# Two-layer graph kernel: tile order at the start, PE transposes for every second node tile, and the MLP's input transposed by DMA as 16-bit halves

## Chip, cores and metric

The kernel runs on one core of one Trainium2 chip. The metric is device time in microseconds (us) of a whole launch; the time before is the median of three runs. The profile is of one further execution of the same program, taken by the hardware profiler. Engines are named as in the profile: PE (TensorE; PEld its weight loads), DVE (VectorE), ACT (ScalarE), POOL (GpSimd), SP (SyncE, which here only issues DMAs).

## What is computed

There are 3327 nodes with 1024 features each, and a weighted adjacency matrix. Cut to what matters, the reference is:

```python
# layer 0: quantised graph convolution
h = relu(layernorm(x))
xq = round(min(h / act_alpha, 1) * 15)
wq = round(clip(((W - mean(W)) / std(W)) / wgt_alpha, -1, 1) * 7)
s = relu(xq @ wq * scale)
x1 = x + scale2 * (adj / adj_scaling_factor) @ round(min(s / act_alpha2, 1) * 15)
# layer 1: graph attention with 8 heads of 64, then an MLP
h = relu(layernorm(x1)); Wh = h @ W_head            # per head
e = leaky_relu(Wh @ a1 [:, None] + Wh @ a2 [None, :], 0.2)
enc = concat_heads(elu(softmax(where(adj > 0, e, -9e15)) @ Wh))     # 3327 x 512
out = x1 + (relu(relu(relu(enc @ W1.T + b1) @ W2.T + b2) @ W3.T + b3) @ W4.T + b4)
```

## The kernel before

The nodes are cut into T = 26 tiles of 128 rows (the last one is short and padded). Each tile lies with its nodes in the 128 partitions, and the kernel runs through four stages, one after the other, with little overlap at the seams.

**First stage (L210 to L450): `xq @ wq`.** `x` comes in by DMA, two tiles to a buffer (`xs`, three buffers). DVE takes a tile's mean and variance (`bn_stats`, L239), a short chain of tiny instructions makes the scale and bias (`normalise`, L258; sqrt on ACT, for later tiles the small products on POOL), ACT normalises, applies relu and rounds to bytes (`to_bytes`, xb, L279), and DVE clamps to a bf16 tile xq (L289). As PE contracts over partitions, xq must be turned so that features lie in the partitions: this is `quantise`. For tile 0 eight PE transposes go into PSUM (L297) and ACT copies them out to `xqt` (L298); for the other 25 tiles SP issues one SBUF-to-SBUF DMA transpose (L300). PE multiplies `xqt` with the quantised weight `w_int` (L423, 16 matmuls of 128x512 to a tile), ACT evicts the result with relu and rounding (sb, L449), and DVE clamps it (s_int, L450). The result's PSUM tiles (mm) have three buffers.

The weight itself must be quantised first. That is a chain: statistics of its eight row blocks (six blocks on DVE at L334, two on ACT at L252 to L256), an aggregate (L359), two tiny matmuls with ones for the mean and the variance over all partitions (L361, L371), a square root on ACT, scale and bias (L162, L163). Then 16 half blocks are rounded to bytes by ACT (L408) or DVE (L406) and clamped by DVE (L412) or POOL (L410). Between those half blocks the program slips the steps of tiles 1 to 5, by the table `between` (L389).

**What sets the order.** Tile's scheduler puts the instructions of each engine in a fixed order when the kernel is built, by its own estimate of when each is ready, and each engine then runs its list in that order; every wait in such a list holds what stands behind it. Instructions given to `tc.keep_in_program_order` (`pin` in the listing) keep their order among themselves. Before, the small steps of `reciprocal`, `scaled` and `normalise` for tile 0 (L112, L117, L131 to L163) are not pinned, and they stand between or behind the weight's first statistics on DVE.

**Second stage (L453 to L555):** adjacency times `s_int`, layer norm, and per tile the heads' products `Wh`. **Third stage (L565 to L854): attention.** For each of 32 rounds (half of the nodes, head; `attends`) DVE builds 0/1 selections `sel` (L826), PE multiplies them with the features (acc, L835) and, between, mask times difference features (mps, L636), whose masks ACT casts (mf, L635) and whose PSUM bank (one buffer) ACT empties (part, L640). The generator `close` finishes a round some steps later, in pieces: adding, scaling, elu; its last piece is a DVE instruction (L697) that leaves 7 (or 6) tiles by 64 columns of `enc` in `ht`, which a DMA on POOL's queue (L701) writes to `enc_d` in DRAM as float32.

**MLP (L738 to L918).** It runs in groups of four tiles, 512 nodes wide (six groups of four and one of two). `load_nodes` (L761) loads a group's `enc` and `x1` with nodes in the partitions, into one of two buffers (nodes0, nodes1), a group ahead. PE transposes `enc` (16 transposes of 128x128 float32, L894), ACT evicts them to `enct` (L897), and three `dense` layers follow (L869, evicted by ACT at L876), then the last layer (o, L906), to which DVE adds `x1` and the bias (L902, L916), and SP stores (L918). Group 0's transposes (L783, L788) and first layer (L793, L801) are slipped into the last attention round by `first_layer`; its weights and biases are loaded there too (L758, L773), into memory that the attention has freed.

Of the kernel before, what the change touches and what calls it, by code (L numbers as in the profile page):

```python
# [8 lines left out]
F32 = mybir.dt.float32  # L9
BF16 = mybir.dt.bfloat16  # L10
F32R = mybir.dt.float32r
U8 = mybir.dt.uint8
I8 = mybir.dt.int8
# [15 lines left out]
HD = 64  # L29
# [30 lines left out]
def two_layer_kernel(  # L60
# [39 lines left out]
    feat_d = dram.tile([T, NH, P, HW], F32, name="feat_d")  # L100
    dsum_d = dram.tile([T, NPAIR, P, HW], F32, name="dsum_d")
    src_d = [dram.tile([NH, len(sub) * P], F32, name=f"src_d{i}") for i, sub in enumerate(SUBS)]
    enc_d = dram.tile([NP, EMB], F32, name="enc_d")

    const.tile([P, 152], F32, name="gap")
    ndst = const.tile([P, T, NH], F32, name="ndst")
    ratio = const.tile([P, T, NH], F32, name="ratio")


    def reciprocal(t, name):  # L110
        r = const.tile([P, 1], F32, name=name)
# [46 lines left out]
    def scale_and_bias(rs, mean, n, factor, tag, engine=nc.vector):  # L158
# [17 lines left out]
    with tc.tile_pool(name="at", bufs=2, reuse_waits="tile") as atp:  # L176
# [34 lines left out]
        w = large(w_life, "w", [P, KF, F])  # L211
        with tc.tile_pool(name="s1", bufs=2, reuse_waits="tile") as s1, tc.tile_pool(
            name="s1_mm", bufs=3, space=PSUM, reuse_waits="tile"
        ) as mm_ps, tc.tile_pool(name="s1_tp", bufs=1, space=PSUM, reuse_waits="tile") as tp_ps:
# [69 lines left out]
            def quantise(t, xb=None, ordered=False):  # L284
                if xb is None:
                    xb = to_bytes(t, ordered)

                xq = s1.tile([P, F], BF16, name="xq")
                ins = nc.vector.tensor_scalar(xq, xb, QA, None, ALU.min)  # L289
                if ordered:  # L290
                    pin(ins)

                xqt = s1.tile([P, KF, P], BF16, name="xqt", bufs=4)
                if t == 0:
                    tp = tp_ps.tile([P, KF, P], BF16, name="tp")
                    for k in range(KF):
                        nc.tensor.transpose(tp[:, k, :], xq[:, k * P : (k + 1) * P], ident_b)  # L297
                    pin(nc.scalar.copy(xqt, tp))  # L298
                else:
                    nc.sync.dma_start_transpose(xqt, xq)  # L300
                return xqt
# [279 lines left out]
    with tc.tile_pool(name="sel", bufs=4, reuse_waits="tile") as selp, tc.tile_pool(  # L581
# [83 lines left out]
        def close(i):  # L665
# [23 lines left out]
            for b in range(nb):  # L689
# [11 lines left out]
            nc.gpsimd.dma_start(  # L701
                enc_d[sub[0] * P : (sub[-1] + 1) * P, h * HD : (h + 1) * HD].rearrange(
                    "(b p) d -> p b d", p=P
                ),
                ht[:, :nb],
            )

        def pin(ins):
            tc.keep_in_program_order(ins)
# [21 lines left out]
        for i, (c, g, e, si) in enumerate(attends):  # L731
            if i == len(attends) - 1:
# [4 lines left out]
                def nodes(name):  # L737
                    n = large(mlp, name, [P, T * HW])  # L738
                    return (
                        n[:, : 4 * EMB].rearrange("p (q e) -> p q e", q=4),  # L740
                        n[:, 4 * EMB : 4 * (EMB + F)].rearrange("p (q e) -> p q e", q=4),
                    )

# [11 lines left out]
                def weight(ap, k, m):  # L755
# [22 lines left out]
                def first_layer():  # L778

                    for k in range(EMB // P):  # L780
                        tp = m_ps.tile([P, 512], F32, tag="mps", name="tp0")
                        for q in range(4):
                            nc.tensor.transpose(  # L783
                                tp[:, q * P : (q + 1) * P],
                                enc_x1[0][0][:, q, k * P : (k + 1) * P],
                                ident,
                            )
# [69 lines left out]
    with tc.tile_pool(name="s4", bufs=2, reuse_waits="tile") as s4, tc.tile_pool(  # L857
# [23 lines left out]
        for g, t0 in enumerate(range(0, T, 4)):  # L881
            tiles = range(t0, min(t0 + 4, T))
            cols = len(tiles) * P
            enc, x1 = enc_x1[g % 2]
            if t0 + 4 < T:
                load_nodes((g + 1) % 2, t0 + 4)
            if g == 0:
                h1 = h1_0
            else:
                enct = s4.tile([P, EMB // P, 512], F32, name="enct")  # L890
                for k in range(EMB // P):
                    tp = ps_p.tile([P, 512], F32, tag="ps", name="tp4")
                    for q, t in enumerate(tiles):
                        nc.tensor.transpose(  # L894
                            tp[:, q * P : (q + 1) * P], enc[:, q, k * P : (k + 1) * P], ident
                        )
# [65 lines left out]
```

## Time and profile before

| | us |
|---|---|
| median of three runs | 2277.46 |
| lowest and highest run | 2276.98, 2278.27 |
| the profiled execution's own time | 2277.77 |
| its span (first to last instruction) | 2276.0 |
| first product of the first stage (L423) | 28.5 |
| last product of the first stage | 134.8 |
| start of group 1's transposes in the MLP (L894) | 2012.7 |

How to read it: times are in us from the span's start, unless marked ns. A line of the timeline is start, duration, engine, source line, operation, `out<-in` with shapes, how many, and in brackets the engine's idle time before it and what ended it. A line of the waits is who waited, for whom, then total us, number of times, and the longest. A line of the chain is start, duration and what ran; the chain is followed back from the last instruction through what released each step. The page's slices cut the span in 40 and give the busy share in tenths. A matmul's duration holds its latency, so two neighbours overlap; the distance of their starts tells what one costs.

### The profile page before, as it was taken

The page shows a single profiled execution, that of the slowest core. Times are in us where ns is not written, and L with a number is a line of the kernel's source. Part 1 is how long each engine was busy: PE and PEld are TensorE (multiplying, and loading weights), DVE is VectorE, ACT ScalarE, POOL GpSimd, SP SyncE. Part 2 cuts the span into 40 slices and gives each one's busy share as a digit, 9 for nine tenths or more (in the row PEclk, how much of TensorE's full clock was granted, in tenths as well). Part 3 has the DMA queues.
Part 4 walks back from the last instruction along what each step waited for, and adds up shares of the span by engine and source line. Part 5 has one row for each costly group of instructions (what it writes and reads, how often), then busy time and mean ns, then how long its engine had stood idle before and what let it go on. Part 6 is the DMA issues. An engine that isn't in the chain of part 4 may idle for free. (4 is left out here: it accounts for less than half of the span.)

```text
span 2276.0 us, 31632 instructions
## 1 busy us (share of the span) xinstructions
PE 2219.2 (98%) x12688; PEld 1772.3 (78%) x12696; DVE 1538.1 (68%) x1963; ACT 978.7 (43%) x1640; POOL 143.6 (6%) x241
## 2 busy tenths in 40 slices
PE   4999999999999999899999999999999999999998
PEld 1467777777777777589999999999999999744444
DVE  7745545555555455487999999999999999732211
ACT  5633333433343333346555555555555555311110
POOL 1300101011010111000000000000000000000000
PEclk9999999999999999999999999999999999999999
DMA  6854444454444544754233141654242422333311
GB/s 208 207 188 134 159 144 159 134 164 151 150 152 139 167 146 152 261 176 137 85 114 112 60 134 55 226 174 149 85 146 84 137 85 75 127 143 126 120 56 56
DMA packets 176579, 311.47 MB, mean 137 GB/s; under 512 B 36452, under 2 KB 117300, under 8 KB 176432
## 3 DMA queue, kind: packets, MB, share of 16 engines
q1 hardware_dynamic: 156648, 236.28, 32.0%
q0 software_dynamic: 19776, 73.17, 10.0%
q8 instruction: 99, 1.62, 0.3%
q14 instruction: 48, 0.39, 0.1%
q10 hardware_dynamic: 8, 0.00, 0.0%
HBM read 216.07 MB, written 86.79 MB: 133 GB/s over the span
## 5 line engine op out<-in xcount | busy, mean ns | idle before, releaser
L826 DVE SCALAR_TENSOR_TENSOR sel<-srow,ndst,mask 128x896 fp32r<-128x896 f32 (+1 forms) x832 | 864.1, 1080 | 51.4 <-PE acc L835 38.7
L636 PE MATMUL mps<-dw,mf 128*128 128x260 f32 x2704 | 454.9, 283 | 0.1
L532 PE MATMUL mm<-s_int,hi 128*128 128x512 f32 x1352 | 432.9, 399 | 0.0
L532 PE MATMUL mm<-s_int,lo 128*128 128x512 f32 x1352 | 421.8, 391 | 0.0
L835 PE MATMUL acc<-f_even,sel 128*128 128x260 f32 x2704 | 397.1, 284 | 0.1
L835 PE MATMUL acc<-f_odd,sel 128*128 128x260 f32 x2704 | 394.5, 286 | 0.0
L635 ACT CAST mf<-mask 128x1664 fp32r<-128x1664 uint8 x208 | 331.3, 1593 | 124.0 <-PE mps L636 101.2
L636 PEld LDWEIGHTS mps<-dw,mf 128*128 128x128 f32 x2704 | 378.2, 188 | 0.3 <-ACT part L640 0.3
L835 PEld LDWEIGHTS acc<-f_odd,sel 128*128 128x128 f32 x2704 | 352.8, 188 | 7.3 <-issue 3.4
L835 PEld LDWEIGHTS acc<-f_even,sel 128*128 128x128 f32 x2704 | 355.1, 188 | 2.9 <-ACT srct L489 0.3
L532 PEld LDWEIGHTS mm<-s_int,lo 128*128 128x128 f32 x1352 | 253.8, 188 | 57.6 <-issue 5.7
L532 PEld LDWEIGHTS mm<-s_int,hi 128*128 128x128 f32 x1352 | 252.1, 188 | 55.7 <-issue 5.7
L192 DVE TENSOR_SCALAR mk<-at 128x896 uint8<-128x896 f32 (+1 forms) x104 | 61.5, 593 | 257.2 <-DMA at<-in_adj_t 256.3
L187 ACT CAST hi<-at 128x896 fp32r<-128x896 f32 x104 | 92.6, 891 | 328.9 <-PE mm L532 294.8
L473 PE MATMUL whm<-whead,ht 128*128 128x512 f32 x416 | 187.1, 603 | 0.8 <-ACT ht L470 0.8
L906 PE MATMUL o<-weights,h 128*128 128x512 f32 x416 | 179.7, 592 | 0.0
L906 PEld LDWEIGHTS o<-weights,h 128*128 128x128 f32 x416 | 79.0, 190 | 99.1 <-issue 98.8
L473 PEld LDWEIGHTS whm<-whead,ht 128*128 128x128 f32 x416 | 77.5, 191 | 98.2 <-issue 88.1
L191 DVE TENSOR_TENSOR lo<-at,hi 128x896 fp32r<-128x896 f32 x104 | 106.6, 1025 | 58.9 <-ACT hi L187 49.4
L640 ACT COPY part<-mps 128x260 f32<-128x260 f32 x104 | 39.2, 377 | 221.5 <-PE mps L636 221.5
L916 DVE TENSOR_TENSOR yo<-o,nodes 128x1024 f32<-128x1024 f32 (+1 forms) x27 | 31.9, 1184 | 138.2 <-PE o L906 138.0
L423 PE MATMUL mm<-w_int,xqt 128*128 128x512 bf16 x408 | 95.4, 386 | 14.8 <-ACT sb L449 4.8
(154 smaller groups left out, 1519.7 us busy)
## 6 DMA issues: line engine op xcount, KB each, us to landing
feat_d<-fw POOLq DMA_DIRECT2D x26, 1040.0 KB, 5.4
f_even<-feat_d SPq DMA_DIRECT2D x7, 3380.0 KB, 13.3
f_odd<-feat_d SPq DMA_DIRECT2D x7, 3380.0 KB, 12.7
at<-in_adj_t SPq DMA_DIRECT2D x52, 448.0 KB, 4.4
at<-in_adj_t SPq DMA_DIRECT2D x52, 384.0 KB, 3.2
mask<-mask_d SPq DMA_DIRECT2D x39, 416.0 KB, 7.4
dw<-dsum_d SPq DMA_DIRECT2D x16, 910.0 KB, 8.8
dsum_d<-dw POOLq DMA_DIRECT2D x26, 520.0 KB, 6.5
```

The lines of the kernel that those rows point to most:

```text
L187: ins = nc.scalar.copy(hi, at)
L191: nc.vector.tensor_tensor(lo, at, hi.bitcast(F32), ALU.subtract)
L192: ins = nc.vector.tensor_scalar(mk[:, r], at, 0.0, None, ALU.is_gt)
L423: nc.tensor.matmul(mm[:, r], xqts[t][:, k, :], w_int[:, k, r], start=(k == 0), stop=(k == KF - 1))
L473: nc.tensor.matmul(whm, ht[:, k, :], whead[:, k, :], start=(k == 0), stop=(k == KF - 1))
L532: nc.tensor.matmul(mm[:, c * 512 : (c + 1) * 512], which[:, q, :], s_int[j][:, c * 512 : (c + 1) * 512], start=(j == 0 and which is hi), s ...
L635: nc.scalar.copy(mf, mask[:, j : j + TH, :])
L636: nc.tensor.matmul(ps, mf[:, j % TH, :], dw[:, j, :], start=(j == 0), stop=(j == T - 1))
L640: nc.scalar.copy(part[:, i % 7], ps.rearrange("p (q c) -> p q c", q=2))
L826: nc.vector.scalar_tensor_tensor(sel[:, :nb], srow[:, :nb], ndst[:, j, h : h + 1], mask[:, :, j, :], ALU.is_gt, ALU.mult,)
L835: nc.tensor.matmul(accs[b], sel[:, b, :], f[:, j, :], start=(j == 0), stop=(j == T - 1))
L906: nc.tensor.matmul(ps[:, c * 512 : (c + 1) * 512], h3[:, k, q * P : (q + 1) * P], w4[:, k, c * 512 : (c + 1) * 512], start=(k == 0), stop= ...
```

## The change

- In the first stage, `reciprocal` and `scaled` are pinned, tile 0's scale and bias are written out as pinned instructions ahead of the weight's statistics, and tile 0's rounding to bytes stands ahead of them too.
- Every tile with an even number is transposed by PE into PSUM and copied out by ACT (two PSUM buffers instead of one); the tiles with odd numbers keep the DMA transpose. The ACT copy is pinned where the tile's other steps are (tiles 0 and 2).
- `enc` goes to DRAM as two planes of 16-bit halves of its float32 words: one more ACT copy in `close` (eh) splits the words, and two DMAs on POOL's queue write them. In the MLP, SP loads each group by two DMA transposes, one of each plane, so that features come to lie in the partitions, and ACT joins the halves to words again: four copies to a group, made in the group before it; for group 0 in `first_layer`. PE's transposes of `enc` go.
- A constant gap in SBUF shrinks by the 32 words that the new small tiles take.

```diff
-    enc_d = dram.tile([NP, EMB], F32, name="enc_d")
-    const.tile([P, 152], F32, name="gap")
+    enc_d = dram.tile([2, NP, EMB], U16, name="enc_d")
+    const.tile([P, 120], F32, name="gap")
...
     def reciprocal(t, name):
-        nc.vector.reciprocal(r, t)
+        tc.keep_in_program_order(nc.vector.reciprocal(r, t))
...
     def scaled(t, c, name):
-        nc.vector.tensor_scalar(r, t, c, None, ALU.mult)
+        tc.keep_in_program_order(nc.vector.tensor_scalar(r, t, c, None, ALU.mult))
...
+    def halves_of_words(words):
+        return words.bitcast(U16).rearrange("p (n two) -> p two n", two=2)
...
-        ) as mm_ps, tc.tile_pool(name="s1_tp", bufs=1, ...) as tp_ps:
+        ) as mm_ps, tc.tile_pool(name="s1_tp", bufs=2, ...) as tp_ps:
...
-                if t == 0:
+                if t % 2 == 0:
                     tp = tp_ps.tile([P, KF, P], BF16, name="tp")
                     for k in range(KF):
                         nc.tensor.transpose(tp[:, k, :], xq[:, k * P : (k + 1) * P], ident_b)
-                    pin(nc.scalar.copy(xqt, tp))
+                    ins = nc.scalar.copy(xqt, tp)
+                    if ordered:
+                        pin(ins)
                 else:
                     nc.sync.dma_start_transpose(xqt, xq)
...
             r_aa = reciprocal(aa_t, "r_aa")
+            pin(nc.vector.tensor_scalar(mv0[:, 0, 1:2], mv0[:, 0, 1:2], EPS, None, ALU.add))
             to_q = scaled(r_aa, 2.0 * QA, "to_q")
-            normalise(xs01, mv0, 0, 1)
+            s0, q0, r0, b0 = (small.tile([P, 1], F32, name=f"x0{c}", bufs=1) for c in "sqrb")
+            v0 = mv0[:, 0, 1:2]
+            pin(nc.scalar.activation(s0, v0, AF.Sqrt))
+            pin(nc.vector.reciprocal(r0, s0))
+            pin(nc.vector.scalar_tensor_tensor(q0, v0, r0, s0, ALU.mult, ALU.add))
+            pin(nc.vector.reciprocal(r0, q0))
+            pin(nc.vector.tensor_scalar(r0, r0, to_q, None, ALU.mult))
+            pin(nc.vector.scalar_tensor_tensor(b0, mv0[:, 0, 0:1], -1.0, r0, ALU.mult, ALU.mult))
+            ready[0] = xs01[0], r0, b0
...
+            xb0 = to_bytes(0, ordered=True)
             weight_statistics(0)
-            xqts = {0: quantise(0, ordered=True)}
+            xqts = {0: quantise(0, xb0, ordered=True)}
...
-            nc.gpsimd.dma_start(enc_d[... rows of sub ..., h * HD : (h + 1) * HD], ht[:, :nb])
+            eh = s3.tile([P, 7, HD], F32, tag="ex", name="eh").rearrange("p b d -> p (b d)")
+            eh = eh.bitcast(U16).rearrange("p (q n) -> p q n", q=2)[:, :, : nb * HD]
+            nc.scalar.copy(eh, halves_of_words(ht[:, :nb].rearrange("p b d -> p (b d)")))
+            for q in range(2):
+                nc.gpsimd.dma_start(enc_d[q, ... rows of sub ..., h * HD : (h + 1) * HD], eh[:, q])
...
+                def by_feature(enc, cols):
+                    k = EMB // P
+                    return enc[:, :, : k * cols].rearrange("p q (k c) -> p q k c", k=k)
                 def load_nodes(i, t0):
-                    for q, t in enumerate(range(t0, min(t0 + 4, T))):
-                        nc.sync.dma_start(enc[:, q, :], enc_d[t * P : (t + 1) * P, :])
+                    rows = slice(t0 * P, min(t0 + 4, T) * P)
+                    for q in range(2):
+                        nc.sync.dma_start_transpose(by_feature(enc, rows.stop - rows.start)[:, q], enc_d[q, rows])
...
                 def first_layer():
                     for k in range(EMB // P):
-                        tp = m_ps.tile([P, 512], F32, tag="mps", name="tp0")
-                        for q in range(4):
-                            nc.tensor.transpose(tp[:, q * P : (q + 1) * P], ..., ident)
-                        nc.scalar.copy(enct0[:, k], tp)
+                        nc.scalar.copy(halves_of_words(enct0[:, k]), by_feature(enc_x1[0][0], 512)[:, :, k])
                         yield
...
+            enct = following if g else None
             if t0 + 4 < T:
                 load_nodes((g + 1) % 2, t0 + 4)
+                following = s4.tile([P, EMB // P, 512], F32, name="enct")
+                n = (min(t0 + 8, T) - t0 - 4) * P
+                for k in range(EMB // P):
+                    nc.scalar.copy(
+                        halves_of_words(following[:, k, :n]),
+                        by_feature(enc_x1[(g + 1) % 2][0], n)[:, :, k],
+                    )
             if g == 0:
                 h1 = h1_0
             else:
-                enct = s4.tile([P, EMB // P, 512], F32, name="enct")
-                for k in range(EMB // P):
-                    tp = ps_p.tile([P, 512], F32, tag="ps", name="tp4")
-                    for q, t in enumerate(tiles):
-                        nc.tensor.transpose(tp[:, q * P : (q + 1) * P], enc[:, q, k * P : (k + 1) * P], ident)
-                    nc.scalar.copy(enct[:, k, :cols], tp[:, :cols])
                 h1 = dense(enct, EMB // P, w1, bb1, D1 // P, cols, "h1")
```

More of the change, by code (lines that the diff above doesn't have):

```diff
@@ L12 @@
 U8 = mybir.dt.uint8
+U16 = mybir.dt.uint16
 I8 = mybir.dt.int8
@@ L213, in two_layer_kernel @@
             name="s1_mm", bufs=3, space=PSUM, reuse_waits="tile"
-        ) as mm_ps, tc.tile_pool(name="s1_tp", bufs=1, space=PSUM, reuse_waits="tile") as tp_ps:
+        ) as mm_ps, tc.tile_pool(name="s1_tp", bufs=2, space=PSUM, reuse_waits="tile") as tp_ps:
             w_int = s1.tile([P, KF, F], BF16, name="w_int", bufs=1)
@@ L700, in close @@
             )
[L701 to L706, printed above, removed]
+            eh = s3.tile([P, 7, HD], F32, tag="ex", name="eh").rearrange("p b d -> p (b d)")
+            eh = eh.bitcast(U16).rearrange("p (q n) -> p q n", q=2)[:, :, : nb * HD]
+            nc.scalar.copy(eh, halves_of_words(ht[:, :nb].rearrange("p b d -> p (b d)")))
+            for q in range(2):
+                nc.gpsimd.dma_start(
+                    enc_d[q, sub[0] * P : (sub[-1] + 1) * P, h * HD : (h + 1) * HD].rearrange(
+                        "(b p) d -> p b d", p=P
+                    ),
+                    eh[:, q].rearrange("p (b d) -> p b d", d=HD),
+                )
         def pin(ins):
@@ L739, in nodes @@
                     return (
-                        n[:, : 4 * EMB].rearrange("p (q e) -> p q e", q=4),
+                        n[:, : 4 * EMB].bitcast(U16).rearrange("p (q r) -> p q r", q=2),
                         n[:, 4 * EMB : 4 * (EMB + F)].rearrange("p (q e) -> p q e", q=4),
@@ L780, in first_layer @@
                     for k in range(EMB // P):
-                        tp = m_ps.tile([P, 512], F32, tag="mps", name="tp0")
-                        for q in range(4):
[L783 to L787, printed above, removed]
-                        nc.scalar.copy(enct0[:, k], tp)
+                        nc.scalar.copy(
+                            halves_of_words(enct0[:, k]), by_feature(enc_x1[0][0], 512)[:, :, k]
+                        )
                         yield
@@ L883, in two_layer_kernel @@
             cols = len(tiles) * P
-            enc, x1 = enc_x1[g % 2]
+            x1 = enc_x1[g % 2][1]
+            enct = following if g else None
             if t0 + 4 < T:
                 load_nodes((g + 1) % 2, t0 + 4)
+                following = s4.tile([P, EMB // P, 512], F32, name="enct")
+                n = (min(t0 + 8, T) - t0 - 4) * P
+                for k in range(EMB // P):
+                    nc.scalar.copy(
+                        halves_of_words(following[:, k, :n]),
+                        by_feature(enc_x1[(g + 1) % 2][0], n)[:, :, k],
+                    )
             if g == 0:
@@ L889, in two_layer_kernel @@
             else:
-                enct = s4.tile([P, EMB // P, 512], F32, name="enct")
-                for k in range(EMB // P):
-                    tp = ps_p.tile([P, 512], F32, tag="ps", name="tp4")
-                    for q, t in enumerate(tiles):
-                        nc.tensor.transpose(
-                            tp[:, q * P : (q + 1) * P], enc[:, q, k * P : (k + 1) * P], ident
-                        )
-                    nc.scalar.copy(enct[:, k, :cols], tp[:, :cols])
                 h1 = dense(enct, EMB // P, w1, bb1, D1 // P, cols, "h1")
```

## Prediction

> **What bounds the kernel now.** I read the page first (shares, slices), then the chain that ended last, then PE's waits by stage, then the timelines of the first 60 us and of the last 350 us. Line numbers are those of the kernel before.
>
> The page gives the span and says that TensorE is the bound: 98% busy, every slice but the first at 8 or 9 tenths.
>
> ```profile
> span 2276.0 us, 31632 instructions
> ...
> PE 2219.2 (98%) x12688; PEld 1772.3 (78%) x12696; DVE 1538.1 (68%) x1963; ACT 978.7 (43%) x1640; POOL 143.6 (6%) x241
> ...
> PE   4999999999999999899999999999999999999998
> ...
> DMA  6854444454444544754233141654242422333311
> ```
>
> So PE work that goes is worth its time, PE work that comes costs its time, and of waits only PE's count. In the first stage (L423, 28.5 to 134.8 us), from the waits of PE between 28 and 135 us (total us, times, longest):
>
> ```profile
> PE mm L423 <- ACT sb L449: 4.8, 5, 2.0
> PE mm L423 <- DVE w_int L412: 4.3, 3, 3.5
> PE mm L423 <- POOL w_int L410: 2.9, 5, 0.9
> PE mm L423 <- DMA xqt<-xq: 2.0, 2, 1.5
> ```
>
> The w_int waits are the quantisation of the weight (28.5 to 48 us). The rest, from 49.5 us on, is 1.5 (DMA) and 3.3 us (ACT; its fifth wait, 1.5 us, ends at 49.5). Ahead of that the timeline of all engines has the chain that starts the stage: tile 0's scale is late, so ACT's statistics of the weight are late, and DVE's aggregate at 22.48 waits for them.
>
> ```profile
> 13.00 0.14 DVE L163 SCALAR_TENSOR_TENSOR l01n<-mv,l01r 128x1 f32<-128x1 f32 x1
> ...
> 13.17 1.24 ACT L279 ACTIVATE xb<-xs,l01n,l01r 128x1024 uint8<-128x1024 f32 x1 [6.34 <-DVE l01n L163]
> ...
> 15.20 1.03 PE L297 MATMUL tp<-ident_b,xq 128*128 128x128 bf16 x8 [8.86 <-DVE xq L289]
> 16.27 1.01 ACT L298 COPY xqt<-tp 128x1024 bf16<-128x1024 bf16 x1 [1.85 <-PE tp L297]
> 17.18 1.06 ACT L252 ACTIVATE junk<-w 128x1024 bf16<-128x1024 f32 x1
> ...
> 22.48 0.51 DVE L359 BATCH_NORM_AGGREGATE w_mv<-w_stats 128x2 f32<-128x78 f32 x1 [3.77 <-ACT junk L256]
> ```
>
> The MLP is PE alone. The chain that ended last (start, us, what) has in each group 1.75 us of transposes, then 17.54 and 27.47 us of products:
>
> ```profile
> 2012.83 1.75 PE tp L894 x16
> 2014.58 17.54 PE h_ps L869 x40
> 2032.12 27.47 PE o L906 x64
> ...
> 2246.61 0.87 PE tp L894 x8
> ```
>
> **What the Trainium skill says.** (1) "ScalarE: Activation LUTs", What ACT_TABLE_LOAD costs: an ACTIVATE with immediates takes 186 ns + 0.833 ns per element, overlapping the next by about 93 ns. The trace agrees: 1012 ns for 1024 elements (L298), the next start 0.91 later. (2) "SBUF — State Buffer", Door 1: steps inside a 16-byte line are free, so a 2-byte write every 4 bytes should not slow down; no row of the trace shows one. (3) "DMA: Bandwidth & Descriptors", Latency and other measured facts: a DMA transpose moves 261 GB/s. The trace's transpose of 256 KB lands 3.1 us after its issue, which fits 1 us of transfer and 2 fixed. (4) "TensorE: Matmul & The Clock Gate", Part 4: a PE transpose takes about 275 ns in context. The trace has that as a latency (273 ns, L894) but the starts are 0.1 us apart, and the trace decides.
>
> **The change part by part.**
>
> *Order at the head.* Tile 0's scale no longer waits behind the weight's first statistics (9.98 us). Every word is read at 6.5; eps, square root (0.2), then five dependent DVE steps at 0.2 to 0.25: bias at 8.1, xb 8.15 to 9.4. xq follows the two statistics of k=0 at 11.2 (before: 14.45), ACT starts the weight at 17.18 − 3.25 = 13.95 (the eight loads landed by 13.0: last issue 5.8 + 7.2), and the aggregate at 19.25. DVE's own work, twelve statistics of 0.61, xq 0.65 and small ones, ends at 18.8, just ahead. **−3.25 us.**
>
> *Tile 2 by PE in the middle of the weight.* The built order has ACT: wb(k0), copy of xqt 2, wb(k1), wb(k3), xb 3, wb(k4), wb(k6). Before, counted in its own times:
>
> ```profile
> 36.76 2.21 ACT L408 ACTIVATE wb<-w,wn,wr 128x512 int8<-128x512 f32 x3
> ...
> 37.93 0.69 DVE L289 TENSOR_SCALAR xq<-xb 128x1024 bf16<-128x1024 uint8 x1
> ...
> 38.88 1.23 ACT L279 ACTIVATE xb<-xs,l02n,l02r 128x1024 uint8<-128x1024 f32 x1
> ...
> 40.01 1.50 ACT L408 ACTIVATE wb<-w,wn,wr 128x512 int8<-128x512 f32 x2
> ```
>
> The copy must wait for xq (38.62) and eight transposes (39.6), so it runs 39.65 to 40.65; wb(k4) ends at 43.9 instead of 40.75. DVE, in order, then has w_int(k4) at 43.95, xq 3, wb(k5), two statistics, the normalise chain (1.65) and wb(k7) at 48.5 instead of 45.94. That is the last byte PE waits for: **+2.5 us**, which the DMA wait saved here (0.6) does not touch. Tile 4's transposes (50.9 to 51.9) fit ahead of tile 3's start, ACT-bound at 52.1. So tile 3 starts 0.7 us earlier than before, not 3.25.
>
> *Tiles 6 to 24 by PE.* Ten sets of eight, starts 0.1 apart: 10 × 0.8 = **+8.0 us** on the bound engine (4 if a weight load hid behind each matmul, 10 with refills). Their twelve DMA transposes cost nothing but SP time and DMA share. ACT gets 1.0 us per pair of tiles: xb 2 × 1.2, sb 2 × 1.05, copy 0.95 make 5.5 of a pair's 7.8 us, so it is not the bound.
>
> *Stalls from tile 3 on*, 4.8 before. The DMA wait should go, and with 0.8 more per pair the sb waits shrink; but each set now stands in PE's queue amid matmuls and waits for xq, behind which every product is queued, and ACT's copy waits on it in turn. I take 1.4 left: **−3.4** (from −4.8 to +5). First stage: −0.7 + 8.0 − 3.4 = +3.9.
>
> *Closing.* 32 copies eh of 896 or 768 words' halves, 0.93 and 0.83 us, and 32 more DMAs on POOL (0.9 each, POOL 6% busy). ACT waits for DVE's L697 in them, with L640 behind, for which PE waits. I set each L697 end against the next L640 start: per unit 2.3, 5.6 and 1.45 us, and in the fourth the order puts L640 first. All fit 1.0: **0**. At 1.45 or more per copy one in four would push PE.
>
> *Group 0 (last attention round).* Removed: 16 transposes, 1.75, and a 0.7 wait. But products of the first layer move into their place (1947.0), and they need w1, issued at 1942.98 (its memory is freed by the last L636) and landing 6.1 later, at 1949.1: 2.1 us of PE lost, partly regained as DVE's selections run on without pause to 1970.3, so PE can end 2.1 us earlier at most. PE's sum: 1949.1 + 132 × 0.12 + 8 × 0.86 = 1971.8 against 1973.4, −1.5; the last eh (0.83) ahead of two h3 evictions gives back 0.5. **−1.0** (−2.4 to +1).
>
> *Groups 1 to 6.* Transposes gone: 5 × 1.75 + 0.87 = **−9.6**. New: four ACT copies per group of 1024 two-byte elements, 1.04 us each (next start 0.95), one group ahead. SP's transposes, two of 512 KB, an estimated 2.5 to issue and 5 to land (twice the 1.23 and the transfer of L300's 256 KB), sit between output stores with 6.9 us a tile. Group 1's must wait for the last close (1985.5 before, about 1989 now): landing 1997, copies 2002, needed 2011; a slack of 9. But the order puts copies of groups 3 to 6 between the evictions of h1 and h2: after h1's last eviction (7.7 us into the group) two copies, h2[0] at 9.6 instead of 9.0, a copy, h2[1] at 11.2 instead of 10.7, so PE waits 0.5, three groups long: **+1.5**.
>
> Sum: +3.9 + 0 − 1.0 − 9.6 + 1.5 = −5.2. The profiled execution took 2277.77 (span 2276.0 and 1.77 around it), 0.3 over the median 2277.46; from the median, **2272.3 us**.
>
> **The rivals.**
> *Slower: the ScalarE copy of halves runs at half rate.* No row shows a 2-byte write at a 4-byte step. At 1.9 us, h2[0] and h2[1] come 1.5 and 1.6 late: 3.1 for three groups and 1.5 for the one of group 6 make +10.8 in place of +1.5, and eh at 1.8 overruns the gap of 1.45 eight times and 2.3 nowhere, +3. 2272.3 + 9.3 + 3 = 2285 (2282 to 2290). It decides from about 1.4 to 1.5 us a copy on. For it: nothing; against it: (2), and rates that don't vary with type. 15%.
> *First-stage stalls stay.* Each set waits for xq as the square root, POOL's steps and xb take some 4.4 us behind sb in ACT's order: with 0.5 us a set, 2272.3 + 5 = 2277 (2275 to 2281). For it: 13.7 us of ACT's idle time there ends with POOL's l02r. 21%.
> *All cover holds.* No stall in the first stage (−1.4), no ACT wait in the MLP (−1.5), group 0 −1.5: 2269 (2266 to 2270). 19%.
> *The transposes from DRAM come late.* Only group 1 has less than a group's slack: up to +3, in the range.
>
> **How the numbers follow.** Forecast 45%, its own range 2270 to 2275.5. About 0.2% (4.6 us) is what a measurement of this kernel can tell from no change: faster means below 2272.9. Faster: the 19 and some 29 of the 45, 48%; same: the other 16 and 20, 36%; slower 16%. 2266 to 2281 leaves out the slower rival and little else.
>
> **What would show it.** Right: the aggregate of the weight at 19.3; tile 3's first product near 48.8; L423's end at 138 to 140; no PE transposes after 1940; a PE wait of about 2 for w1 near 1947; enct copies of 1.04 us; groups of about 45.5 us (before 46.75), the last full one 45.0. Wrong: copies over 1.4 us, products in the first stage waiting for xq through ten sets, or PE waiting for mps after a close.

## The result, and the profile after

The changed kernel takes 2271.75 us (median of 9 runs, 2269.59 to 2273.10), the kernel before 2278.03 (9 runs): ratio 0.9971, 95% interval 0.9961 to 0.9982, so 6.3 us or 0.29% faster. The forecast was 2272.3. The profiled execution of the changed kernel took 2271.88, its span is 2270.1, against 2276.0 before: 5.9 us. Line numbers below are those of the changed kernel, unless an experiment's lines are shown.

The page looks much as before: TensorE at 98%, with 2.3 us less of busy time; the first slice of PE goes from 4 to 5 tenths.

```profile
span 2270.1 us, 31658 instructions
...
PE 2216.9 (98%) x12688; PEld 1767.0 (78%) x12688; DVE 1536.2 (68%) x1963; ACT 1033.3 (46%) x1684; POOL 170.8 (8%) x273
...
PE   5999999999999999899999999999999999999998
```

The first surprise is at the head of the first stage, in the timeline of all engines. The bias of tile 0 comes at 7.84 (before 13.00), VectorE's first statistics of the weight at 7.92 (before 9.98), the aggregate at 17.33 (before 22.48).

```profile
7.84 0.16 DVE L338 SCALAR_TENSOR_TENSOR x0b<-mv,x0r 128x1 f32<-128x1 f32 x1
7.92 1.28 DVE L350 BATCH_NORM_STATS2 w_stats<-w 128x6 f32<-128x512 f32 x2
8.03 1.24 ACT L284 ACTIVATE xb<-xs,x0b,x0r 128x1024 uint8<-128x1024 f32 x1 [1.13 <-DVE x0b L338]
...
12.03 1.06 ACT L257 ACTIVATE junk<-w 128x1024 bf16<-128x1024 f32 x1
...
17.33 0.51 DVE L376 BATCH_NORM_AGGREGATE w_mv<-w_stats 128x2 f32<-128x78 f32 x1 [0.51 <-ACT junk L261]
```

PE's waits of the first stage, 23 to 138 us (total us, times, longest), can be set beside those that the forecast shows for before. The waits for DMA transposes are gone, and of those for sb 0.6 is left; in their place PE waits for xq ahead of its own transposes. A set is the eight transposes of one tile.

```profile
PE tp L302 <- DVE xq L294: 4.5, 4, 2.0
PE mm L440 <- POOL w_int L427: 4.4, 5, 1.9
PE mm L440 <- DVE w_int L429: 3.5, 1, 3.5
PE mm L440 <- ACT xqt L303: 1.1, 1, 1.1
PE mm L440 <- ACT sb L466: 0.6, 1, 0.6
```

PE's timeline from 33 to 96 us places them. Tile 2's set stands at 33.53; the last byte of the weight lets PE go on at 44.31; tile 3 starts at 46.61 (before 49.54). Three later sets wait 0.80, 1.37 and 2.00; the set at 95.48 waits for nothing, and costs the 0.45 us to the next product at 95.93.

```profile
33.53 0.62 PE L302 MATMUL tp<-ident_b,xq 128*128 128x128 bf16 x8
35.26 4.73 PE L440 MATMUL mm<-w_int,xqt 128*128 128x512 bf16 x21 [1.10 <-ACT xqt L303]
...
44.31 0.81 PE L440 MATMUL mm<-w_int,xqt 128*128 128x512 bf16 x3 [1.87 <-POOL w_int L427]
...
46.61 8.11 PE L440 MATMUL mm<-w_int,xqt 128*128 128x512 bf16 x29 [0.59 <-ACT sb L466]
...
64.55 0.62 PE L302 MATMUL tp<-ident_b,xq 128*128 128x128 bf16 x8 [0.80 <-DVE xq L294]
...
70.42 0.62 PE L302 MATMUL tp<-ident_b,xq 128*128 128x128 bf16 x8 [1.37 <-DVE xq L294]
...
79.94 0.62 PE L302 MATMUL tp<-ident_b,xq 128*128 128x128 bf16 x8 [2.00 <-DVE xq L294]
...
95.48 0.61 PE L302 MATMUL tp<-ident_b,xq 128*128 128x128 bf16 x8
```

Stage 2's first product starts at 138.52 (before 134.82), first the line of before, then that of the changed kernel:

```profile
134.82 0.81 PE L532 MATMUL mm<-s_int,hi 128*128 128x512 f32 x2
```

```profile
138.52 0.82 PE L549 MATMUL mm<-s_int,hi 128*128 128x512 f32 x2
```

In the chain that ended last, the MLP has lost its transposes, and in three groups a pair of ScalarE's copies has come into it (in the first of them from 2023.31 to 2025.83, between the products of h1 and those of h2); the groups after those have none.

```profile
2015.82 6.88 PE h_ps L891 x16
2023.31 2.52 ACT enct L913 x2
2026.43 7.19 PE h_ps L891 x16
2033.62 27.47 PE o L928 x64
...
2196.63 17.54 PE h_ps L891 x40
```

The groups take 45.25 to 45.27 us three times and 45.03 and 45.00 in the last two (from one first o product to the next; 46.75 before).

### The profile page after: what moved, and what is told of

It is laid out like the page before. It is cut to its first block, busy times and chain, and to the rows that moved or that the text cites. A ratio compares the mean times of both kernels' runs of the same rounds, so it can differ in the third digit from the quotient of the medians.

```text
span 2270.1 us, 31658 instructions
## 1 busy us (share of the span) xinstructions
PE 2216.9 (98%) x12688; PEld 1767.0 (78%) x12688; DVE 1536.2 (68%) x1963; ACT 1033.3 (46%) x1684; POOL 170.8 (8%) x273
## 4 chain that ended last, share of the span: by engine, by line
PE 52%; ACT 1%; DVE 0%; DMA 0%; issue 0%; DVEq 0%; ACTq 0%
PE acc L857 27%; PE mps L653 13%; PE o L928 8%; PE h_ps L891 4%; ACT enct L913 0%; PE h_ps L815 0%; DMA weights<-in_w1t 0%; ACT h L898 0%; DVE sel L848 0%; DVE nodes L924 0%; ACT su L697 0%; DVE su L694 0%; DVE yo L938 0%; ACT rest L823 0%; DVEq L981 0%
## 5 line engine op out<-in xcount | busy, mean ns | idle before, releaser
L722 POOL DMA_DIRECT2D enc_d<-eh x64 | 57.5, 903 | 942.9 <-ACT eh L720 876.2
```

What stands on the lines that cost most here:

```text
L722: nc.gpsimd.dma_start(enc_d[q, sub[0] * P : (sub[-1] + 1) * P, h * HD : (h + 1) * HD].rearrange("(b p) d -> p b d", p=P), eh[:, q].rearran ...
```

## The experiments

Times are medians; each ratio is to the runs of the kernel before on the same chip (2277.0 to 2278.0). "MLP" stands for the change's second half, with the closing copies and group 0. Edits are cut to what matters, and cuts are marked with dots.

**The MLP alone, first try (m_only).** The changed kernel with the first stage of before: no pins, no tiles of its own for tile 0's scale, tile 0 alone transposed by TensorE, and one PSUM buffer for that.

```
             r = const.tile([P, 1], F32, name=name)
-            tc.keep_in_program_order(nc.vector.reciprocal(r, t))
+            nc.vector.reciprocal(r, t)
...
-                if t % 2 == 0:
+                if t == 0:
```

> The kernel before with the change's second half alone (the encoding written as halves of words, transposed by DMA, joined by ScalarE), first stage untouched. Theory (the traces of before and after compared by stage: group 0 gives 0.6 us, groups 1 to 6 give 8.9): 9.5 us under before, about 2268.5, with first product of stage 2 at 134.8 as before. The forecast on record has 9.1 for these parts. Rival (the first stage and the MLP share something, such as memory placement or throttling, so that the parts don't add): under 7 or over 12 us.

2279.11, ratio 1.0007 (0.9998 to 1.0015): 10 us over what was expected. Stage 2, which no edit touches, took from 134.52 to 957.23, 822.7 us, against 810.3 before. What differed there was where things lie in memory. The change cuts the unused tile named gap from 152 to 120 words, and four tiny tiles take the space that this frees; this kernel had the 120 words without the four tiles, so that all behind it lay 128 bytes off. The next experiment puts the 152 words back.

**The same with the gap at 152 words (m_gap).**

```
-    const.tile([P, 120], F32, name="gap")
+    const.tile([P, 152], F32, name="gap")
```

> The change's MLP alone again, this time with the unused tile named gap at its old 152 words, so that all that is placed behind it lies where it lay in the kernel before (in the first try it had the 120 words of the change without the four small tiles that fill the difference, 128 bytes off). Theory (the 12.4 us that stage 2 took more in the first try, 822.3 for 809.9, come from the 128 bytes alone, through PE's matmuls at 0.233 for 0.228 us): stage 2 takes 810 again, time 9.5 under before, about 2268.0. Rival (something else in the half change slows PE in stage 2, such as the missing order): stage 2 still takes 822, time 2279.

2268.66, ratio 0.9962 (0.9948 to 0.9975), 8.7 us under before. The two kernels differ in nothing but the gap. The answers for the line of stage 2's products (ns min/median/max, first and last start), first m_only's, then m_gap's:

```profile
L539 PE MATMUL mm<-s_int,hi x1352: 387/393/800, 134.5 to 957.0; 128*128 128x512 f32 x194
```

```profile
L539 PE MATMUL mm<-s_int,hi x1352: 387/389/796, 137.7 to 947.8; 128*128 128x512 f32 x194
```

With the 128 bytes a product takes 4 ns more in the median, and the stage 12.4 us more; the granted clock is 1.00 in both from 150 to 950 us, so that is the placement alone. Which operand's address does it isn't shown. The 137.7 is 2.9 us later than before's 134.82, on the same code up to there (m_only: 134.5). Of these, 1.7 are one stretch of products that takes 12.21 us instead of the 10.52 of before, at a granted clock of 0.94 (90 to 115 us). This profiled execution was the slowest of its five runs (2271.01); the other four, 2267.97 to 2269.03, lie 8.4 to 9.4 under before, where 9.5 were expected.

**The first stage alone (hs_only).** The changed kernel with all from the attention on as before.

```
-    enc_d = dram.tile([2, NP, EMB], U16, name="enc_d")
+    enc_d = dram.tile([NP, EMB], F32, name="enc_d")
...
```

> The kernel before with the change's first half alone (fixed order at the head, and every second tile transposed by TensorE). Theory: the first stage costs what the traces show, so 3.7 us over before, about 2281.7; the forecast on record has 3.9. Rival (a later first stage is made up in the stages after it, which then had slack): within 1.5 us of before.

2282.07, ratio 1.0020 (1.0012 to 1.0028): 4.7 over before, where 3.7 were expected. Nothing is made up later; the first stage is a loss by itself. Added up, the two halves alone give −4.1 (m_gap −8.7, hs_only +4.7), and the change gave −6.3; their intervals are some 3 and 2 us wide on either side, so that isn't a contradiction, but it isn't a proof that the halves add either.

**The change without its sets (hm).** Tile 0 alone is transposed by TensorE, and the transposes have one PSUM buffer, as before.

```
-        ) as mm_ps, tc.tile_pool(name="s1_tp", bufs=2, ...) as tp_ps:
+        ) as mm_ps, tc.tile_pool(name="s1_tp", bufs=1, ...) as tp_ps:
...
-                if t % 2 == 0:
+                if t == 0:
```

> The change without its sets of TensorE transposes: fixed order at the head, tile 0 alone transposed by TensorE, all other tiles by DMA as before, MLP as changed. Theory (the head is worth 5.15 us by the trace and nothing in the product phase of before used up that gain): first product at 23.4, stage 2's first product at 129.7, time 5.15 + 9.5 under before, about 2263.4, faster than both kernels. Rival (the stalls for the DMA transposes and for sb, 4.8 us in before, grow when the products start earlier, since the tile loads and transposes don't come earlier): the head gives 1 to 3 us only, 2265.5 to 2267.5. Second rival (the head's gain was luck of one trace, the weight's first slice having landed 2 us earlier): 3.25, so 2265.3.

2262.57, ratio 0.9937 (0.9924 to 0.9949): 14.8 under before, as the first theory has it. First product at 23.27, stage 2 at 128.93. The weight's last byte comes at 41.98, 18.71 after the first product (18.72 in before; with the sets 20.94), and tile 3 starts at 44.28:

```profile
41.98 0.81 PE L440 MATMUL mm<-w_int,xqt 128*128 128x512 bf16 x3 [0.57 <-POOL w_int L427]
44.28 5.99 PE L440 MATMUL mm<-w_int,xqt 128*128 128x512 bf16 x27 [1.49 <-ACT sb L466]
```

From there on its waits of PE (46 to 140 us) are 3.7 us in all, not more than before's 4.8. So the rival, that stalls eat up the gain of the head, isn't borne out:

```profile
PE mm L440 <- ACT sb L466: 2.5, 2, 2.0
PE mm L440 <- DMA xqt<-xq: 1.2, 1, 1.2
```

**The change without its order at the head (sm, then sm_gap with the gap at 152 words).**

> The change without its order at the head: every second tile by TensorE, the MLP as changed, the head's order as before. Theory: the sets and tile 2 cost 8.9 us in the first stage (3.7 net, plus the 5.15 that the head gave), so stage 2's first product at 143.7, time 8.9 - 9.5 against before, about 2277.4. Rival (the sets need the order at the head, or the reverse: with a later start the tiles' statistics are further ahead, so the sets' waits of 4.2 us vanish): about 2273.

> TensorE's sets and the changed MLP with the head's order of before, and the tile named gap at 152 words. Theory (placement cost 12.2 us in the first try): 2288.0 - 12.2, so 2275.8, stage 2 from 142.5. Rival: no change from 2288.

sm: 2288.03 (1.0049, 1.0036 to 1.0061), its stage 2 again 822.6 us long: the placement, not the sets. sm_gap: 2277.85 (1.0002, 0.9994 to 1.0010), stage 2 from 142.55, 810.9 us long. That is the 2277.4 that adding the parts gave for sm; the 2275.8 written for sm_gap is 2 us low, since the time fell by 10.2 and not by the 12.2 that it took off.

**Each set twice (twice).** The second eight transposes of a set write what the first wrote.

```
-                    for k in range(KF):
+                    for k in list(range(KF)) * (2 if t >= 6 else 1):
                         nc.tensor.transpose(tp[:, k, :], xq[:, k * P : (k + 1) * P], ident_b)
```

> The changed kernel with each set of eight TensorE transposes from tile 6 on issued twice into the same tile (ten sets more, the second writes what the first wrote). It prices a set by itself. Theory (the trace of after: 0.45 us of PE a set amid matmuls, weight loads hidden): 4.5 us over the changed kernel if nothing waits, about 2276.3. Rival (0.8 a set as the forecast had it, weight loads not hidden): 8 us, about 2279.8. Second rival (the doubled set sits in stalls that PE has anyway): under 2 us.

2272.80, ratio 0.9980 (0.9973 to 0.9988): 1 to 2 us over the changed kernel, which these intervals can't tell from nothing. So the second rival came true in the time. PE's timeline prices the doubled set at 0.90 us (77.77 to 78.67), so a set at 0.45, half of the forecast's 0.8:

```profile
77.77 1.06 PE L302 MATMUL tp<-ident_b,xq 128*128 128x128 bf16 x16
78.67 7.07 PE L440 MATMUL mm<-w_int,xqt 128*128 128x512 bf16 x31
```

Ten sets more are 4.5 us of PE, yet stage 2 starts at 138.63, against 138.52. Some 1.9 us of it lie where PE waited anyway (its waits for xq from tile 3 on are 2.3 instead of 4.2 us). As much again is the clock: the table of stretches has a granted clock (the third number from the right) of 0.89 at 45 to 60 us and 0.83 at 80 to 90 in the changed kernel, and 1.00 in both here.

```profile
45.00:60.00 15.00, 14.12 (x75) 6.63 (x75) 13.59 (x33) 12.79 (x16) 4.08 (x13) 0.89 0.75 176
...
80.00:90.00 10.00, 10.00 (x51) 4.69 (x52) 7.14 (x17) 6.85 (x9) 3.95 (x12) 0.83 0.61 214
```

```profile
45.00:60.00 15.00, 12.67 (x73) 5.94 (x73) 13.58 (x32) 12.67 (x15) 3.99 (x13) 1.00 0.74 174
...
80.00:90.00 10.00, 9.95 (x59) 5.05 (x59) 6.64 (x17) 7.94 (x9) 2.98 (x14) 1.00 0.56 165
```

In these two stretches of the changed kernel 32 products (two tiles; a few of their records are missing from the trace) take 7.94 us (from 46.61) and 7.73 (from 80.40), instead of the 6.90 from 88.58 on. The rest of the 4.5 isn't accounted for.

**Slice 3 of the weight first (slice3).** hm with one swap.

```
-            weight_statistics(0)
+            weight_statistics(3)
...
-                    weight_statistics(k)
+                    weight_statistics(0 if k == 3 else k)
```

> Fixed order at the head, no sets but tile 0's, MLP by DMA (the kernel that took 2262.6 us), with one swap: VectorE measures slice 3 of the weight first and slice 0 in slice 3's place, as the built order of the kernel before has slice 3 and 4 ahead of slice 0. Theory (of the 5.15 us that the head gave, 3.25 come from tile 0's scale no longer standing behind the statistics, and 1.9 from the first statistics reading the slice that lands first): the first statistics begin at about 10.0 instead of 7.8, xq of tile 0 behind them moves 2 us, the first product comes at 25.2 instead of 23.3, and the time is 1.9 over 2262.6. Rival (slice 0's landing varies from run to run, and the order of slices has no part): the first statistics begin at 7.8 all the same.

2266.33, ratio 0.9947 (0.9933 to 0.9960), 2 to 4 us over hm. The times alone hardly tell that from nothing, but the traces do. The first statistics wait for their slice until 9.79, and the first product comes at 25.06 instead of 23.27:

```profile
9.79 1.29 DVE L350 BATCH_NORM_STATS2 w_stats<-w 128x6 f32<-128x512 f32 x2 [1.55 <-DMA w<-in_w]
```

So the wait until 9.98 in the kernel before, behind which the forecast put the statistics of slice 0, was a wait for slice 3. In the built order of the kernel before, VectorE's statistics read the slices 3, 4, 0, 1, 6, 7; in the changed one 0, 1, 3, 4, 6, 7, and there slice 0 is read without a wait at 7.92. All slices have the same name in the profile. The statistics are pinned in both kernels. So the rule given above, that pinned instructions keep their order among themselves, did not hold in the kernel before; what broke it there isn't shown.

**The pair's small steps on VectorE (norm_dve).** The changed kernel with another engine for the steps from variance to scale.

```
-                normalise(xs, mv, t0, GT, nc.gpsimd)
+                normalise(xs, mv, t0, GT)
```

> The changed kernel with the seven small steps that turn a pair's mean and variance into scale and bias on VectorE instead of GpSimd. Theory (PE's stalls from tile 3 on, about 8 us by arithmetic, are tile quantisation arriving at the pace of its chain of statistics, square root, GpSimd's steps, xb and xq, in which GpSimd's steps with their handoffs take some 3.3 us a pair): a shorter chain brings xq forward, PE's waits for xq go from 4.2 to under 1.5, stage 2 starts at about 135.5 instead of 138.5, 3 us under the changed kernel, 2268.7. Rival (VectorE's order, not the latency of the chain, sets when xq comes; the small steps then only lengthen VectorE's queue): waits for xq the same or longer, 2271.7 or more.

2270.96, ratio 0.9970 (0.9960 to 0.9980): no difference from the changed kernel that can be measured. PE waits 3.8 us for xq in the stage (4.5 in the changed kernel), and 0.7 for a DMA transpose. Stage 2 starts at 136.40, 2.1 us earlier, but 0.8 of that is the clock (no stretch at 0.83 here). The theory, waits for xq under 1.5, isn't borne out.

**The sets later in PE's queue (defer).** The changed kernel with each set from tile 6 on behind the product of the tile four before; in the built order this moves the sets of tile 12 and later.

```
+                if later:
+                    return xq
+                return transposed(t, xq, ordered)
...
+                    later = t >= 2 and t % 2 == 0
+                    xqts[t + 4] = quantise(t + 4, later=later)
...
                 del xqts[t]
+                if t + 4 < T and later:
+                    xqts[t + 4] = transposed(t + 4, xqts[t + 4])
```

> The changed kernel with the TensorE transposes of tiles 6 to 24 issued after the product of the tile four before, not ahead of it; in the built order the sets of tile 12 and later ones stand 12 to 16 matmuls later in PE's queue (2.6 to 3.4 us), those of tiles 6 to 10 where they stood. Theory (a set in PE's queue waits for an xq that is late by a fixed amount, and every product behind it waits along, so standing later hides it): the waits of 1.4 and 2.0 us ahead of the sets of tiles 12 and 14 go, the one of 0.8 ahead of tile 10 stays, stage 2 starts at about 135 instead of 138.5, and the time is 3.4 under the changed kernel, 2268.4. Rival (the loop of products, sb, statistics, xb, xq and set goes round at its own pace, and PE's queue order only moves the place where PE waits): PE's waits for xq, or for the copy xqt in their place, stay over 3.5 us, stage 2 at 138 to 139, time within 1 us of the changed kernel.

2271.73, ratio 0.9975 (0.9964 to 0.9985): no gain, as the rival had it. The waits of 1.37 and 2.00 are gone from their places, and PE waits elsewhere: 1.0 for xq at 101.9 and 2.0 for sb at 104.6.

```profile
PE mm L445 <- ACT sb L474: 2.6, 2, 2.0
PE tp L307 <- DVE xq L294: 2.0, 3, 1.0
```

**The joining copies on VectorE (hm_dve).** hm with the copies of groups 1 to 6 moved, two after the second and two after the third output tile of the group before; VectorE's additions around them are pinned too.

```
-                    nc.scalar.copy(halves_of_words(following[:, k, :n]), ...)
...
+                if q in (1, 2) and t0 + 4 < T:
+                    for k in (2 * q - 2, 2 * q - 1):
+                        pin(nc.vector.tensor_copy(halves_of_words(following[:, k, :n]), ...))
```

> Fixed order at the head, no sets but tile 0's, and the MLP by DMA with the joining copies of groups 1 to 6 on VectorE, two after the second and two after the third output tile of the group before, in a fixed order of VectorE there (ScalarE keeps those of group 0). Theory (ScalarE's copies of 1.33 us make PE wait 0.25 us in three or four groups): 1 us under the kernel with those copies on ScalarE, about 2261.5, groups of 45.0 us all. Rival (a VectorE copy of 1.1 to 2.2 us holds back the eviction of an output tile, two tiles of which PE can run ahead): the groups grow over 45.3 and the time is 2263 or more.

2261.05 (2260.37 to 2261.65), ratio 0.9929 (0.9917 to 0.9942): the fastest kernel, 16.4 us under before and about 10 under the changed one. All full groups take 45.0 us, as the theory had it. VectorE needs 732 ns for what ScalarE does in 1328 (min/median/max, hm_dve's line, then the changed kernel's):

```profile
L939 DVE COPY enct<-nodes x24: 445/732/735, 1993.8 to 2226.1; 128x1024 uint16<-128x1024 uint16 x20, 128x512 uint16<-128x512 uint16 x4
```

```profile
L913 ACT COPY enct<-nodes x24: 752/1328/1345, 1998.1 to 2161.5; 128x1024 uint16<-128x1024 uint16 x20, 128x512 uint16<-128x512 uint16 x4
```

Against hm its median is 1.5 us lower and the span of its trace 0.4 longer, which is less than these can tell apart; that PE's waits of 0.25 are gone is read from the groups.

**Group 0's copies on GpSimd (best1).** hm_dve with one more edit.

```
-                        nc.scalar.copy(
+                        nc.gpsimd.tensor_copy(
                             halves_of_words(enct0[:, k]), ...
```

> The fastest kernel so far (order at the head, no sets but tile 0's, joining copies of groups 1 to 6 on VectorE; 2261.05 us) with the four joining copies of group 0 on GpSimd instead of ScalarE. Theory (ScalarE's copies of 1.3 us stand ahead of the evictions of the last attention sums and make PE wait 1.1 us): that wait goes, 2260.0. Rival (GpSimd's copy of 1024 two-byte elements takes 2 us or more, and the first layer of group 0 waits for it): PE waits more than 1 us at the first layer, 2261 or more.

2265.98, ratio 0.9945 (0.9932 to 0.9959): a miss, about 4 us slower than hm_dve, and by a third mechanism. In the traces it is 4.6, but 1.4 of these are lost in the first stage, which the edit doesn't touch (stage 2 starts at 130.52 instead of 129.1, with a granted clock of 0.83 at 80 to 90 us). The other 3.2 are lost in the last attention round. The wait for xs is gone, but PE waits 2.9 us for VectorE's selections. GpSimd's four copies run from 1936.58 to 1943.83, and what VectorE runs beside them takes twice its time: three selections of 768 elements, 2.0 to 2.1 us each (the fourth of the row comes later and takes 1.0), and the addition of two SBUF tiles into md. VectorE's groups, of best1 at 1931 to 1945, then of hm_dve at 1928 to 1945 (busy us, mean ns):

```profile
L848 DVE SCALAR_TENSOR_TENSOR sel<-srow,ndst,mask 128x768 fp32r<-128x768 f32 x4 | 7.1, 1803 | 0.0
...
L661 DVE TENSOR_TENSOR md<-part 128x780 f32<-128x780 f32 x1 | 2.1, 2057 | 0.0
```

```profile
L848 DVE SCALAR_TENSOR_TENSOR sel<-srow,ndst,mask 128x768 fp32r<-128x768 f32 x8 | 7.9, 1009 | 0.2 <-PE acc L857 0.2
...
L661 DVE TENSOR_TENSOR md<-part 128x780 f32<-128x780 f32 x1 | 1.0, 973 | 0.7 <-ACT part L657 0.7
```

This fits the Trainium skill, "SBUF — State Buffer", SBUF: two separate sides: VectorE and GpSimd share a pair of ports under an exclusive lock, which a VectorE operation with two SBUF inputs needs against a GpSimd operation that reads SBUF. A selection reads three tensors, and each of the four VectorE operations grows by about 1 us. From the second on GpSimd's copies start 2.0 us apart, as VectorE's operations do, as if the two took turns; so the copies' mean of 1.81 us (the first takes 1.35) may hold waiting of their own. The lock itself is in no row.

## Why the prediction was right, and where its steps were not

The sum was 5.2 us, 5.9 were measured in the two traces, 6.3 in the medians. The sign and the size are right. For the MLP the steps carry this; in the first stage they don't: the order at the head, the sets and the stalls were each off by 2 to 3.5 us, and together with a lower clock (+1.9), which the forecast didn't have, the errors cancel. That the stage came out at +3.7 for +3.9 is luck. In us, from the traces of before and after:

| step | forecast | measured |
| --- | --- | --- |
| order at the head | −3.25 | −5.15 (aggregate 22.48 to 17.33) |
| tile 2 amid the weight | +2.5 | +2.2 (20.94 − 18.72) |
| ten sets | +8.0 | +4.5 (10 × 0.45) |
| stalls from tile 3 on | −3.4 | −0.6 (4.8 to 4.2), clock +1.9, unlisted rest +0.8 |
| first stage | +3.9 | +3.7 (134.82 to 138.52) |
| closing | 0 | 0 |
| group 0 | −1.0 | −0.6 |
| groups 1 to 6 | −8.1 | −8.9 |

The medians of the experiments say the same of the large parts, in differences from before: the order at the head is worth −6.1 without the sets (hm less m_gap) and −6.7 with them (the change less sm_gap), and the sets cost +8.5 with the order at the head (the change less hm) and +9.2 without it (sm_gap less m_gap). Each of these can be off by some 3 to 4 us.

*Order at the head: mechanism right, size short.* The step said that xq moves by 3.25 because it "follows the two statistics of k=0 at 11.2". It follows them at 9.31. The forecast took the label "DMA w" on the wait until 9.98 for the landing of slice 0; the built order and slice3 show that it was slice 3's, and that the other 1.8 us (25.06 − 23.27) hang on the order of the slices, which the fixed order changes too.

*Tile 2: right.* The copy of xqt waits for xq and PE's transposes, and the bytes of the weight behind it on ScalarE are late; hm takes it away and has 18.71 again. Tile 3 started 2.9 earlier instead of 0.7 since the head gave 1.9 more and this step cost 0.3 less.

*Ten sets: mis-sized.* The forecast priced a set by starts 0.1 us apart, as they are at the head and in the MLP of before, and named 4 us as the low end "if a weight load hid behind each matmul". Amid products eight transposes take 0.45 us (twice: sixteen take 0.90). The 275 ns of the Trainium skill ("TensorE: Matmul & The Clock Gate", Part 4) are five times the spacing of 0.056 us here; to let the trace decide was right, but it was the wrong row of it.

*Stalls: wrong.* "The DMA wait should go" holds, and so does the fall of the sb waits; but "1.4 left" doesn't, 4.2 are. The set that stands in PE's queue waits for xq, as the rival said: it is that rival that came true, at about half of the 5 us that it took (2.8 more than forecast), and the cheaper sets (3.5 less) paid for it. What paces xq isn't settled. The small steps on VectorE instead of GpSimd don't help (norm_dve), so the rival's account by POOL's steps isn't borne out, and sets later in the queue only move the wait to other places (defer, 4.6 us with those for sb, against 4.8). That speaks for a loop of products, sb, statistics, xb and xq that goes round at its own pace, in which PE has some slack (twice hides 1.9 us in it); which member sets the pace was not isolated. What brings the clock of 0.89 and 0.83 in two stretches (1.9 us) isn't shown. Sets aren't needed for it: slice3 and hm_dve, without them, have the 0.89 and best1 the 0.83; nor do they always bring it: twice has 1.00 in both stretches. But of the traces with sets six of seven have the 0.89, and of those without two of seven, so that sets make it likelier can't be ruled out.

*Closing: right.* The copies take 0.83 and 0.94 us as said, and from stage 2's first product to the last products of mps it is 1806.9 us before (to 1941.67) and 1806.8 after (to 1945.28); PE never waits for mps after a close.

*Group 0: right within its range.* PE's waits are 1.1 for w1 (forecast 2.1) and 1.0 for the evictions xs, for which the forecast had nothing: three of the four copies, 1.3 us each, stand ahead of them on ScalarE (1944.29 to 1948.35).

*Groups 1 to 6: right; the copy mis-sized in one direction, its effect in the other.* The copy takes 1.33 us, not 1.04, and PE waits 0.25 in three groups, not 0.5 (45.26 against 45.02): sum −9.6 + 0.75. The copies stand where the forecast put them, those of groups 1 and 2 while PE is busy with o, those of groups 3 to 6 between the evictions of h1 and h2. Where these are of full length (groups 3 to 5), the first eviction of h2 comes 9.9 us into the group instead of the 9.6 forecast (8.8 where no copy stands), but only 0.25 of the delay reaches PE. The 1.33 stayed just under the 1.4 to 1.5 us from which the slower rival decided. Group 1's transposes landed by 1998.1, its copies began there, and were needed at 2015.8; the fourth rival had nothing to stand on.

## What to carry to other kernels

A change of three parts that moves the time by 0.3% can hold parts worth −15 and +9 us: hm, which is the change less its sets, is worth more than twice the change. A wait is named by its tile, not by the slice of it: where a scheduler orders several readers of one tile, look in the built order which slice comes first before you take its landing as given. And when parts are tried alone, what lies behind them in memory has to stay where it was, or 128 bytes are measured in place of the part.

## What the runs showed that was not expected

- 128 bytes of placement made 2704 products of stage 2 slower by some 1.5%: 822.7 for 810.3 us, the same in two pairs of kernels that differ in nothing else (m_only and m_gap, sm and sm_gap).
- ScalarE's copy of 1024 two-byte elements costs 1.33 us where it writes every other half word (752 ns for 512, so 1.12 ns an element), but 0.94 us for 896 where it only reads so and writes in one run: the 186 ns + 0.833 ns an element of the Trainium skill, "ScalarE: Activation LUTs", What ACT_TABLE_LOAD costs. So the stepped write costs and the stepped read doesn't, where the forecast's second citation had a step inside a 16-byte line as free; the measurement decides. VectorE does the same write in 0.73 us.
- Beside GpSimd's copies VectorE's three-input selections took 2.0 to 2.1 us instead of 1.0.
- The first stage of one and the same code ends at 134.5, 134.8 or 137.7 us: a difference of 2 us there needs more than one trace.
